# Layer 1's last scalings among layer 2's first products, in a written order

## The chip, the cores and the metric

The kernel runs on one core of a Trainium2 chip. A core has a matrix engine (TensorE, PE in the profile; its weight loads are PEld), a vector engine (VectorE, DVE), a scalar engine (ScalarE, ACT), a general engine (GpSimd, POOL) and a queue for transfers (SyncE, SP). Each engine works through its own queue in order and waits for the others by semaphores. The metric is the device time of one execution in microseconds (us).

## The reference

Four graph layers work on `x` of shape (8, 2048, 64) with one adjacency matrix of 2048 by 2048 nodes, each followed by a residual addition and a layer norm without weights. The change touches the end of layer 1 and layer 2:

```python
x = _layernorm(x + _L1_gnn_ref(x, ...))      # layer 1: a softmax over neighbours for each feature
# layer 2
A = (adj > 0); deg = A.sum(axis=1)
agg = einsum('ij,bjf->bif', A, x) / max(deg, 1)
out = relu(x @ W_self + b_self + agg @ W_neigh + b_neigh)
out = layernorm(out) * ln_gamma + ln_beta
x = _layernorm(x + out)
```

A layer norm here is a scale and a shift for each row of 64 values: x * rstd + nmr, with rstd and nmr worked out from the row's mean and variance.

## The kernel before

**Tiles.** The 2048 nodes lie in 16 tiles of 128 nodes. `X[:, t]` holds tile t: 128 partitions by 8 batches by 64 features. Nodes are sorted so that tiles 0 to 7 get their neighbour sums from products with the dense matrix `ET` ("by matrix"), and tiles 8 to 15 from gathered rows ("by list").

**End of layer 1 (L801 to L964).** The sums of a tile go to `finish` (L823), which divides on VectorE, adds to X and, when both tiles of a pair (2k, 2k+1) are done, calls `layer_norm` (L185). This takes the statistics on VectorE (`norm_stats`, L162: 8 `bn_stats`, then a chain of ten small instructions) and then scales on ScalarE (`normed`, L178): one activation of 128 by 64 for each tile and batch, 16 for a pair, at L183. Tiles 3 to 7 go through `add_rows` (L817), lists through `add_edges` (L946). The list tiles run from 15 down to 8, the matrix tiles up to 7, so that tiles 8 and 7 end last.

**Layer 2's first products (L1115 to L1133).** For each tile in the order of `turns` (0, 1, 2, 15, 14, 3, 4, 13, 12, 5, 6, 11, 10, 7, 9, 8): TensorE turns the tile in four transposes (`transposed`, L124) into a PSUM tile `pt`, ScalarE copies it to `xT` (L129), and TensorE multiplies it with the two weight matrices side by side (L1120) into a PSUM tile `py`. Half of that is x @ W_neigh, which ScalarE copies out as `y` (L1124). It goes to the table `ytab` in DRAM by SP (L1125), from which the lists' rows are gathered, and is split in three bf16 pieces `Y`: the high one is a cast on GpSimd (L1126), VectorE takes the remainder `rest` (L1130), the middle one is a cast of that on ScalarE (L1131), the low one a difference on GpSimd (L1132). The other half plus the biases becomes `S` (L1127, VectorE). At the end of each tile, `X[:, t]` gets layer 2's beta added (L1133, VectorE), since both the residual and the output need it later.

**Layer 2's main loop (L1280 to L1304).** It has 128 steps k, one for each pair of a matrix tile `it` and a tile `jt` of neighbours. A step issues three products with the pieces of Y (L1290), then what stands `beside` it: the weights of layer 3's heads are prepared at k = 2, 6, 10 and 14 (`prepare`, L1051: VectorE subtracts in place at L1055, TensorE multiplies and transposes at L1057 to L1061, VectorE copies out). Then it moves on the `chains` (L1174), generators that normalise finished tiles and end in `show` (L1213), which copies a tile on GpSimd (L1216) and stores it for layer 3. Between the steps lists are added (`add_edges`, L1262) and the next gathers are issued on GpSimd (`fetch`, L1253). The sum of tile 0 is complete at k = 15 and goes to `finish` (L1230).

**What sets the order.** Outside blocks marked `tc.manual_schedule(engines=...)` a planner orders each engine's instructions by its own estimate of when they can run, with earlier lines preferred. Inside such a block the order of each engine among the block's own instructions is that of the program. The planner may still put instructions from outside the block, also those of other blocks, between them. Before, L1115 to L1133 are in no such block, and the main loop is in one. PSUM has 8 banks: the seam uses 2 for `ps_m`, 2 for `pt` and 4 for two `py`.

Of the kernel before, what the change touches and what calls it, by code (L numbers as in the profile page):

```python
# [21 lines left out]
F32 = mybir.dt.float32  # L22
# [26 lines left out]
def kernel(ctx: ExitStack, tc: tile.TileContext, ins: dict, out: bass.AP):  # L49
    nc = tc.nc  # L50
    x, adj = ins["x"], ins["adj"]
    B, N, D = x.shape
    NT = N // P
    BD = B * D
    NP = B // 2
# [68 lines left out]
    def transposed(dst, src, psp):  # L124

        pt = psp.tile([P, NP, P], F32, name="pt")
        for p in range(NP):
            nc.tensor.transpose(pt[:, p], src[:, 2 * p:2 * p + 2, :].rearrange("p b d -> p (b d)"), ident)
        nc.scalar.copy(dst, pt)  # L129
# [32 lines left out]
    def norm_stats(chunks):  # L162

        n = len(chunks)
        st = small.tile([P, n, NP, 6], F32, name=f"st{n}")

        for c, v in enumerate(chunks):
            for a in range(NP):
                nc.vector.bn_stats(st[:, c, a], v[:, 2 * a:2 * a + 2, :].rearrange("p b d -> p d b"))
        triples = st.rearrange("p n a (k m) -> p (n a k) m", m=3)  # L170
        var, rstd, tmp, nmr = (small.tile([P, n * B], F32, name=f"ln_{k}{n}") for k in "vrtm")
        nc.vector.scalar_tensor_tensor(var, triples[:, :, 2], 1.0 / D, eps.to_broadcast(var.shape),
                                       op0=ALU.mult, op1=ALU.add)
        inv_sqrt(rstd, var, tmp)
        nc.vector.scalar_tensor_tensor(nmr, triples[:, :, 1], -1.0, rstd, op0=ALU.mult, op1=ALU.mult)  # L175
        return rstd, nmr

    def normed(chunks, stats):  # L178
        rstd, nmr = stats
        for c, v in enumerate(chunks):  # L180
            for b in range(B):
                k = c * B + b
                nc.scalar.activation(v[:, b], v[:, b], AF.Identity, scale=rstd[:, k:k + 1], bias=nmr[:, k:k + 1])  # L183
# [120 lines left out]
    def node_products(t0, wk, ps):  # L304
# [24 lines left out]
        for q, ph in enumerate(held):  # L329
# [40 lines left out]
                                   op0=ALU.is_equal, op1=ALU.mult)  # L370
# [184 lines left out]
    wk = adj_.enter_context(tc.tile_pool(name="l0k", bufs=2, reuse_waits="tile"))  # L555
# [220 lines left out]
    engines = {mybir.EngineType.PE, mybir.EngineType.Activation, mybir.EngineType.DVE, mybir.EngineType.Pool}  # L776
# [21 lines left out]

    with ExitStack() as l1:  # L801
        wp = l1.enter_context(tc.tile_pool(name="l1w", bufs=1, reuse_waits="tile"))
        wk = l1.enter_context(tc.tile_pool(name="l1k", bufs=2, reuse_waits="tile"))
        pa = l1.enter_context(tc.tile_pool(name="l1pa", bufs=8, space=PSUM, reuse_waits="tile"))
# [14 lines left out]
                                     start=(jt == 0 and q == 0), stop=(jt == NT - 1 and q == 2))  # L819

        done = set()

        def finish(it, po):  # L823
            for h in range(2):
                rec = wk.tile([P, HB * D], F32, name="rec")
                nc.vector.reciprocal(rec, po[h][:, 0])  # L826
                nc.vector.tensor_tensor(po[h][:, 1], po[h][:, 1], rec, ALU.mult)
                Xs = X[:, it, h * HB:(h + 1) * HB, :].rearrange("p b d -> p (b d)")
                nc.vector.tensor_tensor(Xs, po[h][:, 1], Xs, ALU.add)
            done.add(it)  # L830
            if it ^ 1 in done:
                layer_norm([X[:, t] for t in (it & ~1, it | 1)], wk)


        FIRST = 3
# [8 lines left out]
        rs_, rests = {}, {}  # L844
# [141 lines left out]
    ps_m = None  # L986
# [97 lines left out]
    with ExitStack() as l2:  # L1084
        wp = l2.enter_context(tc.tile_pool(name="l2w", bufs=1, reuse_waits="tile"))
        wk = l2.enter_context(tc.tile_pool(name="l2k", bufs=2, reuse_waits="tile"))
        ps_m = l2.enter_context(tc.tile_pool(name="l2pm", bufs=2, space=PSUM, reuse_waits="tile"))

        Wsn = wp.tile([P, 2, P], F32, name="Wsn")
        nc.gpsimd.memset(Wsn, 0.0)  # L1090
        for k, w in enumerate(("L2_gnn_W_self", "L2_gnn_W_neigh")):
# [6 lines left out]
        b2 = rows("b2", ins["L2_gnn_ln_beta"], wp)  # L1098
# [11 lines left out]
        turns = sorted(range(NT), key=lambda t: turns.index(t) if t in turns else NT)  # L1110
        with ExitStack() as turned:
            tk = turned.enter_context(tc.tile_pool(name="l2t", bufs=2, reuse_waits="tile"))
            ps = turned.enter_context(tc.tile_pool(name="l2ps", bufs=2, space=PSUM, reuse_waits="tile"))
            pa = turned.enter_context(tc.tile_pool(name="l2py", bufs=2, space=PSUM, reuse_waits="tile"))
            for t in turns:  # L1115
                xT = tk.tile([P, NP, P], F32, name="xT")
                transposed(xT, X[:, t], ps)
                py = pa.tile([P, NP, 2, P], F32, name="py")
                for p in range(NP):
                    nc.tensor.matmul(py[:, p].rearrange("p a n -> p (a n)"), xT[:, p],  # L1120
                                     Wsn.rearrange("p a n -> p (a n)"), start=True, stop=True)
                hi, mid, lo = (Y[:, t, k] for k in range(3))
                y = tk.tile([P, NP, P], F32, name="y", bufs=3)
                nc.scalar.copy(y, py[:, :, 1])  # L1124
                nc.sync.dma_start(ytab[t * P:(t + 1) * P, :], y.rearrange("p a n -> p (a n)"))  # L1125
                nc.gpsimd.tensor_copy(hi, y)  # L1126
                nc.vector.tensor_tensor(S[:, t].rearrange("p (q b) d -> p q b d", b=2), py[:, :, 0].rearrange("p q (b d) -> p q b d", d=D),  # L1127
                                        over(bsn, [P, NP, 2, D]), ALU.add)
                rest = tk.tile([P, NP, P], F32, name="rest", bufs=3)
                nc.vector.tensor_tensor(rest, py[:, :, 1], hi, ALU.subtract)  # L1130
                nc.scalar.copy(mid, rest)  # L1131
                nc.gpsimd.tensor_tensor(lo, rest, mid, ALU.subtract)  # L1132
# [146 lines left out]
        engines = {mybir.EngineType.PE, mybir.EngineType.Activation, mybir.EngineType.DVE, mybir.EngineType.Pool}  # L1279
        with tc.manual_schedule(engines=engines):  # L1280
            fetch(0)
            fetch(1)
            selection(0)
            selection(1)
            n = 0
            for k, (it, jt) in enumerate(steps):
                if jt == 0:
                    sums[it] = pa.tile([P, BD], F32, name="pa")
                for q in range(3):
                    nc.tensor.matmul(sums[it], ET[:, jt, it * P:(it + 1) * P], Y[:, jt, q].rearrange("p a n -> p (a n)"),  # L1290
                                     start=(jt == 0 and q == 0), stop=(jt == NT - 1 and q == 2))
                if jt == NT - 1:
                    finish(it)
                if k in beside:
                    f, *a = beside[k]
                    f(*a)
                for _ in range(2 if k % 2 == 0 else 1):
                    advance()
                while n < len(quads) and n * (len(steps) - LATE - EARLY) <= (k - LATE) * len(quads):
                    add_edges(n)  # L1300
                    fetch(n + 2)
                    n += 1
            while chains:
                advance()  # L1304
# [25 lines left out]
    with early, ExitStack() as heads:  # L1330
        wk = heads.enter_context(tc.tile_pool(name="f3s", bufs=2, reuse_waits="tile"))
# [258 lines left out]
        engines = {mybir.EngineType.PE, mybir.EngineType.Activation, mybir.EngineType.DVE, mybir.EngineType.Pool}  # L1590
        AHEAD = 8
        with tc.manual_schedule(engines=engines):
# [11 lines left out]
            for m in range(len(steps) // 2):  # L1604
                it, j = divmod(m, PER)
# [24 lines left out]
            t = NT - 1  # L1630
# [293 lines left out]
    with tc.If(bad > 0), ExitStack() as anyway:  # L1924
# [12 lines left out]
        X = main.tile([P, NT, B, D], F32, name="X")  # L1937
# [13 lines left out]
        with tc.tile_pool(name="adjp", bufs=3) as ap_, tc.tile_pool(name="adjps", bufs=4, space=PSUM) as aps:  # L1951
# [509 lines left out]
```

## Time and profile before

| | us |
|---|---|
| median of 3 runs | 1612.18 |
| lowest and highest run | 1601.11, 1620.49 |
| the profiled execution's own time | 1768.37 |
| its span | 1766.6 |
| last products of layer 1 end | 669.4 |
| first transpose for layer 2 | 669.3 |
| first product of layer 2 (L1120) | 684.5 |
| first product of the main loop (L1290) | 728.4 |
| last product of the main loop | 878 |

Times inside the profile count from the start of the span. A row of the timeline gives start, length, engine, line, operation, output and inputs, shape and count of merged instructions, and in brackets how long the engine had been idle and what released it. In merged rows the length covers all instructions of the row.

### The profile page before, as it was taken

How to read it: one execution, taken by the hardware profiler on the slowest of the kernel's cores; microseconds unless marked ns; L12 is line 12 of the kernel's file. 1: busy time of each engine (PE TensorE's matmuls, PEld its weight loads, DVE VectorE, ACT ScalarE, POOL GpSimd, SP SyncE). 2: the span in 40 equal slices, each digit the busy share in tenths (PEclk: the TensorE clock that was granted, in tenths of full speed). 3: DMA queues.
4: the chain of work that ended last, by engine and by line, in shares of the span. 5: the costliest groups of instructions: out<-in, count | busy, mean ns of one | idle time of the engine just before them, and what ended most of it. 6: DMA issues, size and time to landing. Idle time of an engine off the chain costs nothing.

```text
span 1766.6 us, 39998 instructions
## 1 busy us (share of the span) xinstructions
PE 1409.4 (80%) x16140; PEld 956.7 (54%) x16140; DVE 1165.4 (66%) x2846; ACT 884.2 (50%) x1843; POOL 790.0 (45%) x786
## 2 busy tenths in 40 slices
PE   4775567755899996989728999998989679889884
PEld 4764233322343334522227777777777567777773
DVE  6787578776985646655834666666666536656667
ACT  4553245558833225445634565656555324555564
POOL 1234666661235552656433333343333156666651
PEclk9965575676899998999958999999999879888997
DMA  5434767662247971366434565656565365666651
GB/s 166 126 127 131 211 214 232 179 195 82 102 167 262 328 273 43 128 176 182 123 90 106 151 178 152 172 154 167 161 161 153 89 202 167 179 174 177 181 163 45
DMA packets 159322, 285.71 MB, mean 162 GB/s; under 512 B 68986, under 2 KB 94586, under 8 KB 157050
## 3 DMA queue, kind: packets, MB, share of 16 engines
q0 software_dynamic: 56320, 190.10, 36.5%
q1 hardware_dynamic: 86168, 88.78, 16.8%
q10 hardware_dynamic: 16640, 4.20, 1.0%
q8 instruction: 129, 2.11, 0.5%
q14 instruction: 65, 0.53, 0.1%
HBM read 242.52 MB, written 40.48 MB: 160 GB/s over the span
## 4 chain that ended last, share of the span: by engine, by line
PE 50%; DVE 9%; ACT 6%; issue 4%; DMA 1%; POOL 1%; another core or an unknown queue 1%; SPq 0%; POOLq 0%; ACTq 0%; DVEq 0%
PE pscore L1388 10%; PE po L1413 6%; PE pa L817 6%; PE ps L1716 4%; PE po L1755 4%; PE pt L1693 3%; PE pa L946 2%; PE pscore L1351 2%; PE pa L1290 2%; PE py L1120 2%; PE pscore L1480 2%; PE pe L1686 2%; PE pt L1000 2%; ACT w L1391 1%; DVE w_mid L1394 1%
## 5 line engine op out<-in xcount | busy, mean ns | idle before, releaser
L218 POOL DMA_INDIRECT xs<-xtab,src x160 | 171.8, 1074 | 280.8 <-PE po L1413 241.6
L218 POOL DMA_INDIRECT hs<-ktab,src x160 | 158.5, 991 | 140.2 <-DMA utab<-hT 47.7
L218 POOL DMA_INDIRECT hs<-htab,src x160 | 157.1, 982 | 88.5 <-issue 43.3
L1388 PE MATMUL pscore<-U,xsT 64*128 64x64 f32 (+2 forms) x2560 | 165.8, 280 | 1.1 <-ACT xsT L1375 1.1
L1388 PEld LDWEIGHTS pscore<-U,xsT 64*128 64x128 f32 x2560 | 155.2, 193 | 5.2 <-ACT xsT L1375 1.3
L1391 ACT ACTIVATE w<-pscore 128x512 f32<-128x512 f32 (+1 forms) x128 | 75.8, 622 | 139.7 <-PE pscore L1388 139.3
L1394 DVE SCALAR_TENSOR_TENSOR w<-w,Sel 128x512 f32<-128x512 f32 (+1 forms) x128 | 89.3, 722 | 79.2 <-ACT w L1391 61.1
L183 ACT ACTIVATE X<-X,ln_m,ln_r 128x64 f32<-128x64 f32 x240 | 81.4, 427 | 73.5 <-DVE ln_m L175 59.5
L1755 PE MATMUL po<-hs,w 128*32 128x65 f32 x2048 | 89.4, 236 | 32.3 <-issue 23.4
L1716 PE MATMUL ps<-U,hsT 128*128 128x64 f32 x768 | 104.5, 287 | 8.8 <-issue 5.8
L1716 PEld LDWEIGHTS ps<-U,hsT 128*128 128x128 f32 x768 | 103.0, 210 | 9.8 <-issue 6.0
L218 POOL DMA_INDIRECT rs<-rtab,src x80 | 75.9, 949 | 69.9 <-PE pa L946 47.5
L613 DVE TENSOR_TENSOR hs<-hs,w 128x1024 f32<-128x1024 f32 x80 | 96.7, 1213 | 11.1 <-ACT w L603 6.0
L817 PE MATMUL pa<-R,ET 128*128 128x512 bf16 x440 | 101.6, 380 | 0.0
L826 DVE RECIPROCAL rec<-pa 128x256 f32<-128x256 f32 x32 | 54.4, 1734 | 65.7 <-PE pa L946 41.6
L1755 PEld LDWEIGHTS po<-hs,w 128*32 128x32 f32 x2048 | 71.5, 119 | 45.1 <-issue 33.3
L1413 PE MATMUL po<-w,xs 128*64 128x64 f32 (+1 forms) x2048 | 84.4, 230 | 9.6 <-DVE o L1397 5.6
L218 POOL DMA_INDIRECT rs<-ytab,src x80 | 76.2, 953 | 35.0 <-issue 17.4
L1694 ACT COPY hsT<-pt 128x512 f32<-128x512 f32 x96 | 52.5, 586 | 77.8 <-remote 45.0
L1413 PEld LDWEIGHTS po<-w,xs 128*64 128x64 f32 x2048 | 71.4, 139 | 35.5 <-DVE w L1394 20.4
L1803 ACT ACTIVATE z<-z,ln_m,ln_r 128x64 f32<-128x64 f32 x240 | 83.4, 432 | 12.9 <-DVE ln_m L1791 12.9
L1290 PE MATMUL pa<-Y,ET 128*128 128x512 bf16 x384 | 89.4, 382 | 0.0
(673 smaller groups left out, 3355.3 us busy)
## 6 DMA issues: line engine op xcount, KB each, us to landing
at<-in_adj SPq DMA_DIRECT2D x16, 1024.0 KB
R<-itab SPq DMA_DIRECT2D x60, 256.0 KB
rtab<-r SPq DMA_DIRECT2D x16, 512.0 KB
ptab<-hp SPq DMA_DIRECT2D x16, 384.0 KB
hi<-ptab SPq DMA_DIRECT2D x16, 384.0 KB
htab<-H SPq DMA_DIRECT2D x16, 260.0 KB
own<-htab SPq DMA_DIRECT2D x16, 260.0 KB
ktab<-hb SPq DMA_DIRECT2D x16, 260.0 KB
```

The costliest lines, as they stand in the source:

```text
L183: nc.scalar.activation(v[:, b], v[:, b], AF.Identity, scale=rstd[:, k:k + 1], bias=nmr[:, k:k + 1])
L218: nc.gpsimd.indirect_dma_start(out=dst, out_offset=None, in_=table[:, :], in_offset=bass.IndirectOffsetOnAxis(ap=src[:, it, s, g:g + 1], a ...
L613: nc.vector.tensor_tensor(wx, wx, along(w[:, rows_]), ALU.mult)
L817: nc.tensor.matmul(po[h].rearrange("p a f -> p (a f)"), ET[:, jt, it * P:(it + 1) * P], piece[jt][q][:, h * BD:(h + 1) * BD], start=(jt == ...
L1290: nc.tensor.matmul(sums[it], ET[:, jt, it * P:(it + 1) * P], Y[:, jt, q].rearrange("p a n -> p (a n)"), start=(jt == 0 and q == 0), stop=( ...
L1388: nc.tensor.matmul(pscore[:, k_, f0:f0 + HN * ni].rearrange("p (h i) -> p h i", i=ni), xsT[half, p], Us[it][half, p, :, i0:i0 + ni], start ...
L1391: nc.scalar.activation(w.rearrange("p k a h i -> p k (a h i)"), pscore[:, :, 0:NP * HN * ni], AF.Exp)
L1394: nc.vector.scalar_tensor_tensor(wt, wt, 3.0e38, edge, op0=ALU.min, op1=ALU.mult)
L1413: nc.tensor.matmul(po[half, p, :, a - blk * GB:b - blk * GB], xs[:, f0:f0 + D], w[:, k_, p, :, a - WINDOWS[s][0]:b - WINDOWS[s][0]], start ...
L1716: nc.tensor.matmul(pscore[:, g, 2 * p:2 * p + 2], hsT[:, g, p], U[:, p, :, node_block(g, k)], start=False, stop=(p == NP - 1))
L1755: nc.tensor.matmul(po[node_block(g, k), j, b], w[:, g, t], hs[:, g, t], start=(s == BEGIN[k] and b == 0), stop=(s == END[k] and b == B // ...
L1803: nc.scalar.activation(v, v, AF.Identity, scale=r, bias=n)
```

## The change

The pools and the order of the seam are rewritten:

- `finish` of layer 1 now calls `norm_stats` and `normed` itself. When the tile that completes a pair is in `LATE_NORMS` (6, 7, 8, 9), the statistics are taken as before, but the scalings are put off in the list `late`.
- The loop over `turns` stands in a `manual_schedule` block. It is cut into `turn_x` (transposes and copy), `both_products`, `top_piece` (y, its store, the high piece, S, the remainder) and `other_pieces` (middle and low piece). A step i issues `turn_x` for tile i+1, the products and top piece of tile i, and the other pieces of tile i-1. From the third step on it issues four of the put-off scalings, by turns on ScalarE and VectorE.
- `py` has three buffers in place of two (6 banks) and comes first in PSUM; `ps_m` is opened after the seam, no longer beside it.
- Beta is added to `X[:, turns[k]]` in step k of the main loop, for k from 0 to 15, after what stands beside the step.

The instructions are the same in kind and number but for 16 of the 32 put-off scalings, which go from ScalarE's activation to VectorE's `tensor_scalar`.

```diff
+    late = []
...
         done = set()
+        LATE_NORMS = (6, 7, 8, 9)
...
             if it ^ 1 in done:
-                layer_norm([X[:, t] for t in (it & ~1, it | 1)], wk)
+                pair = it & ~1, it | 1
+                pair_stats = norm_stats([X[:, t] for t in pair])
+                if it in LATE_NORMS:
+                    late.append((pair, pair_stats))
+                else:
+                    normed([X[:, t] for t in pair], pair_stats)
...
-        ps_m = l2.enter_context(tc.tile_pool(name="l2pm", bufs=2, space=PSUM, reuse_waits="tile"))
...
+            pa = turned.enter_context(tc.tile_pool(name="l2py", bufs=3, space=PSUM, reuse_waits="tile"))
             ps = turned.enter_context(tc.tile_pool(name="l2ps", bufs=2, space=PSUM, reuse_waits="tile"))
-            pa = turned.enter_context(tc.tile_pool(name="l2py", bufs=2, space=PSUM, reuse_waits="tile"))
-            for t in turns:
-                xT = tk.tile([P, NP, P], F32, name="xT")
-                transposed(xT, X[:, t], ps)
...
+            def turn_x(t):
+                xTs_[t] = tk.tile([P, NP, P], F32, name="xT")
+                transposed(xTs_[t], X[:, t], ps)
+
+            def both_products(t):
...
+            def top_piece(t):
+                py = pys.pop(t)
                 y = tk.tile([P, NP, P], F32, name="y", bufs=3)
                 nc.scalar.copy(y, py[:, :, 1])
                 nc.sync.dma_start(ytab[t * P:(t + 1) * P, :], y.rearrange("p a n -> p (a n)"))
-                nc.gpsimd.tensor_copy(hi, y)
+                nc.gpsimd.tensor_copy(Y[:, t, 0], y)
...
+                rest = rests[t] = tk.tile([P, NP, P], F32, name="rest", bufs=3)
+                nc.vector.tensor_tensor(rest, py[:, :, 1], Y[:, t, 0], ALU.subtract)
+
+            def other_pieces(t):
+                rest = rests.pop(t)
+                nc.scalar.copy(Y[:, t, 1], rest)
+                nc.gpsimd.tensor_tensor(Y[:, t, 2], rest, Y[:, t, 1], ALU.subtract)
+
+            scalings = [(t, k * B + b, b, stats_) for pair, stats_ in late for k, t in enumerate(pair) for b in range(B)]
+
+            def scale_late(on_dve):
+                t, c, b, (rstd, nmr) = scalings.pop(0)
+                v = X[:, t, b]
+                if on_dve:
+                    nc.vector.tensor_scalar(v, v, rstd[:, c:c + 1], nmr[:, c:c + 1], op0=ALU.mult, op1=ALU.add)
+                else:
+                    nc.scalar.activation(v, v, AF.Identity, scale=rstd[:, c:c + 1], bias=nmr[:, c:c + 1])
+
+            with tc.manual_schedule(engines=engines):
+                turn_x(turns[0])
+                for i, t in enumerate(turns):
+                    if i + 1 < NT:
+                        turn_x(turns[i + 1])
+                    both_products(t)
+                    top_piece(t)
+                    if i:
+                        other_pieces(turns[i - 1])
+                    for k in range(4):
+                        if i >= 2 and scalings:
+                            scale_late(k % 2)
+                other_pieces(turns[-1])
+
+        ps_m = l2.enter_context(tc.tile_pool(name="l2pm", bufs=2, space=PSUM, reuse_waits="tile"))
...
-                nc.vector.tensor_tensor(X[:, t], X[:, t], over(b2, [P, B, D]), ALU.add)
...
+                if k < NT:
+                    nc.vector.tensor_tensor(X[:, turns[k]], X[:, turns[k]], over(b2, [P, B, D]), ALU.add)
```

More of the change, by code (lines that the diff above doesn't have):

```diff
@@ L1110 @@
         turns = sorted(range(NT), key=lambda t: turns.index(t) if t in turns else NT)
+        engines = {mybir.EngineType.PE, mybir.EngineType.Activation, mybir.EngineType.DVE, mybir.EngineType.Pool}
         with ExitStack() as turned:
             tk = turned.enter_context(tc.tile_pool(name="l2t", bufs=2, reuse_waits="tile"))
+            pa = turned.enter_context(tc.tile_pool(name="l2py", bufs=3, space=PSUM, reuse_waits="tile"))
             ps = turned.enter_context(tc.tile_pool(name="l2ps", bufs=2, space=PSUM, reuse_waits="tile"))
-            pa = turned.enter_context(tc.tile_pool(name="l2py", bufs=2, space=PSUM, reuse_waits="tile"))
-            for t in turns:
-                xT = tk.tile([P, NP, P], F32, name="xT")
-                transposed(xT, X[:, t], ps)
-                py = pa.tile([P, NP, 2, P], F32, name="py")
+            xTs_, pys, rests = {}, {}, {}
+            def turn_x(t):
+                xTs_[t] = tk.tile([P, NP, P], F32, name="xT")
+                transposed(xTs_[t], X[:, t], ps)
+            def both_products(t):
+                xT = xTs_.pop(t)
+                py = pys[t] = pa.tile([P, NP, 2, P], F32, name="py")
                 for p in range(NP):
@@ L1121 @@
                                      Wsn.rearrange("p a n -> p (a n)"), start=True, stop=True)
-                hi, mid, lo = (Y[:, t, k] for k in range(3))
+            def top_piece(t):
+                py = pys.pop(t)
                 y = tk.tile([P, NP, P], F32, name="y", bufs=3)
@@ L1125 @@
                 nc.sync.dma_start(ytab[t * P:(t + 1) * P, :], y.rearrange("p a n -> p (a n)"))
-                nc.gpsimd.tensor_copy(hi, y)
+                nc.gpsimd.tensor_copy(Y[:, t, 0], y)
                 nc.vector.tensor_tensor(S[:, t].rearrange("p (q b) d -> p q b d", b=2), py[:, :, 0].rearrange("p q (b d) -> p q b d", d=D),
                                         over(bsn, [P, NP, 2, D]), ALU.add)
[L1129 to L1132, printed above, removed]
-                nc.vector.tensor_tensor(X[:, t], X[:, t], over(b2, [P, B, D]), ALU.add)
+                rest = rests[t] = tk.tile([P, NP, P], F32, name="rest", bufs=3)
[26 more added lines that the diff above has]
+        ps_m = l2.enter_context(tc.tile_pool(name="l2pm", bufs=2, space=PSUM, reuse_waits="tile"))
         gk = l2.enter_context(tc.tile_pool(name="l2g", bufs=8, reuse_waits="tile"))
```

## The prediction

> **What bounds the kernel now.** I read four views, from wide to narrow. First the page's row of engine shares and its chain of the work that ended last. They say that TensorE carries about half of the chain, and that layer 2's first products are 2% of it:
>
> ```profile
> PE 1409.4 (80%) x16140; PEld 956.7 (54%) x16140; DVE 1165.4 (66%) x2846; ACT 884.2 (50%) x1843; POOL 790.0 (45%) x786
> PE 50%; DVE 9%; ACT 6%; issue 4%; DMA 1%; POOL 1%; another core or an unknown queue 1%; SPq 0%; POOLq 0%; ACTq 0%; DVEq 0%
> ```
>
> A share of the whole span says little about one seam, so next the busy times by stretch, in two parts of the seam between the layers (columns: stretch, its length, then busy time of PE, PEld, DVE, ACT, POOL, the granted clock, DMA). In the first part TensorE does 1 us of 15; in the second it does 38 of 44:
>
> ```profile
> 669.30:684.40 15.10, 1.02 (x9) 0.78 (x7) 9.28 (x37) 11.21 (x34) 0.00 (x0) 0.70 0.01 3
> 684.40:728.40 44.00, 38.01 (x185) 32.00 (x186) 30.34 (x44) 24.03 (x44) 27.78 (x29) 0.95 0.23 85
> ```
>
> Then the timeline of the seam. These rows are ScalarE, TensorE and VectorE there (start, length, engine, line, work, count, idle before and its releaser):
>
> ```profile
> 669.29 1.04 PE L128 MATMUL pt<-ident,X 128*128 128x128 f32 x8
> 673.19 10.71 ACT L183 ACTIVATE X<-X,ln_m,ln_r 128x64 f32<-128x64 f32 x32 [15.16 <-DVE ln_m L175]
> 683.81 1.04 ACT L129 COPY xT<-pt 128x512 f32<-128x512 f32 x2
> 684.47 5.97 PE L1120 MATMUL py<-Wsn,xT 128*128 128x256 f32 x16 [14.15 <-ACT xT L129]
> ...
> 695.68 1.04 PE L128 MATMUL pt<-ident,X 128*128 128x128 f32 x8
> 697.57 3.72 PE L1120 MATMUL py<-Wsn,xT 128*128 128x256 f32 x16 [0.85 <-ACT xT L129]
> 701.12 1.04 PE L128 MATMUL pt<-ident,X 128*128 128x128 f32 x8
> ...
> 728.36 2.10 PE L1290 MATMUL pa<-Y,ET 128*128 128x512 bf16 x9
> ```
>
> Two tiles are already transposed at 670.3, but their copy out of PSUM stands on ScalarE behind layer 1's last 32 scalings, which wait for the statistics of the last tile. So TensorE idles 14.15 us. After that the tiles go in pairs, 701.12 - 695.68 = 5.44 us a pair: 1.0 us of transposes, 0.85 us waiting for ScalarE's copy, 3.55 us of products. From the first transpose to the first product of the main loop (L1290): 15.18 us, 5.81 us for the first pair, 7 x 5.44 us, in all 59.07 us.
>
> Last, the list of waits in and after the seam:
>
> ```profile
> PE py L1120 <- ACT xT L129: 20.1, 8, 14.1
> ACT y L1124 <- PE py L1120: 18.4, 16, 3.4
> POOL Xo L1216 <- ACT X L1157: 6.8, 1, 6.8
> ```
>
> The first is the idle time just told. The third is where the next margin lies: a copy on GpSimd, behind which gathers are queued, waits for tile 0's whole normalisation, and TensorE later idles 4.79 us (758.2 to 763.0) for those gathers.
>
> **What the Trainium skill says.** "TensorE: Matmul & The Clock Gate", the section on the clock gate: an idle window of about 3.4 us halves the clock until activity has lasted as long again. The trace agrees: the granted clock is 0.70 in the idle part, and the first 16 products take 5.97 us, later ones 3.72. "PSUM — Partial Sum Buffer", the section on bank collisions: two engines may not read one bank in the same partitions at once, so ScalarE's y and VectorE's S from one product tile go one after the other. The trace agrees: y ends at 688.85, S starts at 688.88. "SBUF — State Buffer", the section on who interferes with whom: a VectorE instruction with two SBUF inputs, or in a 2-port mode, shuts out a GpSimd one that reads SBUF, and the other way round. The trace agrees in size: the addition of beta (L1133) takes 0.69 or 1.03 us, GpSimd's cast (L1126) 0.61 or 0.95.
>
> **The change part by part.**
>
> *Scalings deferred.* Tile 7 completes pair (6,7), tile 8 completes pair (8,9); both are in the late set, and no other pair is. So exactly the 32 activations of the 10.71 us row leave ScalarE's queue ahead of the copies. They come back in eight steps (the third to the tenth tile), two on ScalarE at 10.71/32 = 0.335 us and two on VectorE at 0.31 us (median of the like scaling at L1167). The two engines have room, see below. Tiles 8, 9, 6 and 7 are scaled in steps 3-4, 5-6, 7-8 and 9-10, before their transposes are issued (tile 6 with step 10, the others later), so no transpose waits for them. If that cover were gone, 16 x 0.335 = 5.4 us of ScalarE would lie open.
>
> *The start.* The first copy can run at once, ScalarE being idle since 658: transpose 0.5 us, copy 0.59, two hand-overs of 0.1, so products begin about 1.3 us after the first transpose instead of 15.18. But VectorE is busy with tile 7's finish and its statistics until 677.5, the first remainder (`rest`) stands behind that, and in the new fixed order ScalarE's second step waits for that remainder ahead of the copy for the fourth tile. Products of the first three tiles end near 677.3; the fourth starts at 677.8 if the remainder slips in between the statistics, at about 680-681 if not. I take a bubble of 2.0 us, bounds 0 and 3.5.
>
> *The steps.* The transposes of tile i+1 go ahead of the products of tile i, so the 0.85 us wait is covered by 1.8 us of products. Per tile: TensorE 0.52 + 1.78 = 2.30 us. ScalarE three copies or casts at 0.52 (back to back) + 0.67 = 2.2. VectorE 0.6 + 0.6 + 0.62 = 1.8. GpSimd 0.61 to 0.95 for the cast + 1.16 for the difference = 1.8 to 2.1. TensorE is the longest, so 16 x 2.30 = 36.8 us. The ends: 2.30, and 2.72 if collisions of VectorE's scalings with GpSimd eat the 0.2 to 0.5 us of room. The third buffer for the products covers the time until VectorE has read a tile (about 2.1 us after its products).
>
> Sum of the stage: 1.3 + 2.0 + 36.8 = 40.1 us against 59.07, a gain of **19.0 us**.
>
> *Beta moved.* 16 additions of 0.605 us (two back to back take 1.29) leave the seam, where they stood on VectorE beside TensorE's work and cost nothing, and go into the first 16 steps of the main loop, each of which is only 0.65 us of TensorE. There they are not covered: the preparation of a head (L1055 to L1063) is issued at steps 2, 6, 10 and 14, and TensorE's L1057 waits for VectorE's L1055, which now stands behind four additions. From one L1057 to the next took 3.03 us (730.30 to 733.33). Now: copies done after 1.05 us, four additions 2.42, two L1055 0.5, hand-over 0.1, together 4.1 us. So three times 1.05, and about 0.4 at the first one, whose PSUM bank was held by the last product tile until its remainder is read: **3.6 us** back. Bounds: 1 us (some additions hoisted by the planner) and 6 us (additions slowed to 1.03 by GpSimd).
>
> *Tile 0's chain.* Two additions more stand before tile 0's first statistics are turned into a scale: 1.2 us later, and the 4.79 us wait grows by as much: **1.2 us**, bounds 0 and 3. Behind it on GpSimd's queue are the gathers, and TensorE waits for those. SP's stores of y keep their place: each is issued after its copy and none is waited for before the loop's gathers, which GpSimd still begins after its last low piece.
>
> Net: 19.0 - 3.6 - 1.2 = **14.2 us** of the profiled execution's 1768.37 us (span 1766.6). That execution is 9.7% longer than the runs' median of 1612.18, so I shrink the gain by the same ratio, 0.912: 13 us, **1599 us**. The runs of before lie within 1601 to 1620, so about 1% is what can be told from no change.
>
> **The rivals.** (a) *Nothing is given back*: VectorE's additions fit into waits that TensorE has anyway and there is no bubble; gain 21 x 0.912 = 19, 1593 us. For it: TensorE waits 4.79 us at 758-763 in any case, and a delay before that could vanish in it; against: that wait hangs on tile 0's chain, which is late by as much. (b) *The round of four engines sets the pace*: still 2.72 us a tile, 43.5 + 3.3 = 46.8, gain 12.3 - 4.8 = 7.5, times 0.912 is 7: 1605 us. For it: fixed order, strict queues, GpSimd at 1.8 to 2.1 of 2.3. (c) *Slower*: the fixed order closes a ring in ScalarE's queue: products, y, GpSimd's cast, remainder, middle piece, scalings, the copy for the tile after next, products. Its links add to about 6.3 us (1.8 + 0.6 + 0.95 + 0.7 + 0.6 + 0.67 + 0.6 + 0.4 of hand-overs) and it spans three tiles, so 2.1 us a tile, under 2.30. If a wait ties it to one tile and a half, a step is 4.2 us: 67 + 3 + 4.8 against 59, a loss of 16, 1627 us. It decides from (59.07 - 3.3 - 4.8)/16 = 3.2 us a step. (d) *It doesn't do what it says*: the planner merges the new order with what surrounds it so that the copies still stand late; 1612.
>
> **How the numbers follow.** Forecast 0.50, (a) 0.22, (b) 0.15, (c) 0.08, (d) 0.05. Below 1596 lie most of (a) and the forecast's better end: faster 0.31; slower takes (c) and the spread of the runs: 0.10; same 0.59. The range, 1587 to 1612, goes from (a) less the spread of a median to (b) and (d).
>
> **What would show it.** Right: products start within 3 us of the first transpose; none of the 32 scalings ahead of the first copy; TensorE's wait for the copy near zero from the fourth tile on; 2.3 us a tile; L1290 begins near 710; L1057 spaced near 4.1 us with waits on VectorE. Wrong: a tile at 2.7 us or more, scalings grown by collisions, or a wait for gathers that grows by more than 3 us.

## The result and the profile after

The changed kernel takes 1594.73 us (median of 12 runs, 1590.73 to 1602.76), the kernel before 1605.66 us (12 runs beside it, 1600.52 to 1620.49). The ratio is 0.992, with a 95% interval of 0.9895 to 0.9944: 9 to 17 us faster, 12.8 us in the middle (the two medians alone are 10.9 us apart). The prediction said 13 us and 1599 us; it counted the 1599 from a median of 1612.18 us over three runs.

The kernel before was profiled in an execution of 1768 us, which is as long as its runs beside all the experiments below (medians 1765 to 1779 us) but about 160 us longer than the runs compared here, with 41 us of the difference in layer 0 and 116 us behind layer 2, where nothing was changed, so the traces are compared by stretch and not by their whole spans.

These are the sums for layer 1, for the seam and for layer 2's main loop, of before and then of after (columns as in the prediction; the last one is GB/s moved):

```profile
442.50:669.40 226.90, 218.53 (x1154) 84.58 (x1154) 155.62 (x320) 88.54 (x174) 94.99 (x99) 0.97 0.62 220
669.40:728.40 59.00, 38.93 (x194) 32.68 (x193) 39.52 (x81) 35.24 (x77) 27.78 (x29) 0.88 0.18 64
728.40:878.40 150.00, 134.72 (x611) 46.69 (x613) 92.60 (x321) 77.57 (x208) 88.74 (x97) 0.95 0.58 165
```

```profile
401.20:628.10 226.90, 216.28 (x1152) 83.63 (x1151) 154.59 (x320) 88.58 (x174) 95.86 (x99) 0.98 0.61 220
628.10:670.30 42.20, 37.06 (x192) 31.90 (x192) 34.99 (x83) 29.16 (x62) 24.48 (x29) 0.96 0.26 94
670.30:818.60 148.30, 131.01 (x610) 45.61 (x610) 99.13 (x333) 77.18 (x208) 89.85 (x98) 0.95 0.57 166
```

Layer 1 is 226.9 us in both. The change shows in the second row, the seam: 59.0 us became 42.2 us, while TensorE's busy time in it fell only from 38.9 to 37.1 us. The main loop of layer 2 has 148.3 us in place of 150.0.

The timeline of the seam in the changed kernel, TensorE first and then one step of ScalarE (`xT` is the copy of the next tile, `y` and `Y` the pieces of this and the last one, L1158 two of the put-off scalings):

```profile
632.59 1.77 PE L128 MATMUL pt<-ident,X 128*128 128x128 f32 x8 [4.52 <-DVE X L831]
634.23 2.94 PE L1131 MATMUL py<-Wsn,xT 128*128 128x256 f32 x8
...
646.10 1.93 PE L1131 MATMUL py<-Wsn,xT 128*128 128x256 f32 x8
647.87 0.60 PE L128 MATMUL pt<-ident,X 128*128 128x128 f32 x4
648.31 1.89 PE L1131 MATMUL py<-Wsn,xT 128*128 128x256 f32 x8
...
670.32 2.12 PE L1330 MATMUL pa<-Y,ET 128*128 128x512 bf16 x9 [0.40 <-DVE rest L1143]
```

```profile
645.91 0.59 ACT L1137 COPY y<-py 128x512 f32<-128x512 f32 x1
646.39 0.62 ACT L1147 CAST Y<-rest 128x512 bf16<-128x512 f32 x1
646.91 0.77 ACT L1158 ACTIVATE X<-X,ln_m,ln_r 128x64 f32<-128x64 f32 x2
647.59 0.57 ACT L129 COPY xT<-pt 128x512 f32<-128x512 f32 x1
648.12 0.59 ACT L1137 COPY y<-py 128x512 f32<-128x512 f32 x1
```

The block of 32 scalings is gone, and a tile takes 648.31 - 646.10 = 2.2 us with no wait for a copy. ScalarE has no gap in such a step. New is the first row: TensorE idles 4.52 us *before* the first transposes, where before it idled 14.15 us behind them. It waits for tile 7's last addition on VectorE (L831).

Behind the seam, TensorE at the preparations of the heads in the main loop and at the later wait for gathers, then VectorE at the same preparations. Before:

```profile
728.36 2.10 PE L1290 MATMUL pa<-Y,ET 128*128 128x512 bf16 x9
730.30 0.38 PE L1057 MATMUL pm<-wb 128*128 128x128 f32 x2
733.33 0.39 PE L1057 MATMUL pm<-wb 128*128 128x128 f32 x2
...
739.38 0.38 PE L1057 MATMUL pm<-wb 128*128 128x128 f32 x2
763.00 5.24 PE L1270 MATMUL pa<-rs,self__5913 128*32 128x512 f32 x8 [4.79 <-DMA rs<-ytab,src]
```

After:

```profile
672.27 0.38 PE L1064 MATMUL pm<-wb 128*128 128x128 f32 x2
676.72 0.49 PE L1064 MATMUL pm<-wb 128*128 128x128 f32 x2 [1.26 <-DVE wb L1062]
681.15 0.49 PE L1064 MATMUL pm<-wb 128*128 128x128 f32 x2 [1.13 <-DVE wb L1062]
685.43 0.49 PE L1064 MATMUL pm<-wb 128*128 128x128 f32 x2 [0.98 <-DVE wb L1062]
707.59 4.80 PE L1310 MATMUL pa<-rs,self__5900 128*32 128x512 f32 x8 [3.45 <-DMA rs<-ytab,src]
```

```profile
673.32 2.91 DVE L1338 TENSOR_TENSOR X<-X,b 128x512 f32<-128x512 f32 x4
676.15 0.52 DVE L1062 TENSOR_SCALAR wb<-wb 64x64 f32<-64x64 f32 x2
```

The preparations are 4.3 to 4.45 us apart (3.03 before), and the second to fourth wait for the subtraction that stands behind four additions of beta. The fourth comes 15.11 us after the loop's first product, before it was 11.02. The wait for gathers ends 37.27 us after that product, before 34.64: so 2.6 us of the seam's 16.7 are given back by then, and 14.1 us are left at that point.

At the end of the main loop those 2.6 us are no longer to be seen: from the end of layer 1 to there the rows above give 209.0 and 190.5 us, 18.5 us less, and the changed kernel of experiment 5 gives 193.3. But the loop's length differs by 3.4 us between two profiles of one and the same kernel (148.7 us in experiment 6, 152.1 in experiment 12). So the traces don't show how much of the 2.6 us reaches the whole time.

### The profile page after: what moved, and what is told of

Read it like the earlier page. It is cut to its first block, busy times and chain, and to the rows that moved or that the text cites. A ratio compares the mean times of both kernels' runs of the same rounds, so it can differ in the third digit from the quotient of the medians.

```text
span 1590.5 us, 39997 instructions
## 1 busy us (share of the span) xinstructions
PE 1320.9 (83%) x16140; PEld 911.1 (57%) x16140; DVE 1167.3 (73%) x2862; ACT 884.6 (56%) x1827; POOL 787.3 (50%) x786
## 4 chain that ended last, share of the span: by engine, by line
PE 48%; DVE 12%; ACT 5%; issue 3%; POOL 2%; DMA 1%; SPq 0%; POOLq 0%; ACTq 0%; DVEq 0%
PE pscore L1430 10%; PE pa L818 6%; PE po L1455 6%; PE pscore L1393 4%; PE pt L1007 3%; PE pa L953 3%; PE ps L1758 3%; PE po L1797 2%; PE pscore L1522 2%; PE pt L1735 2%; ACT z L1197 2%; PE pa L889 1%; PE py L1131 1%; ACT X L1197 1%; POOL hs L218 1%
## 5 line engine op out<-in xcount | busy, mean ns | idle before, releaser
L218 POOL DMA_INDIRECT xs<-xtab,src x160 | 168.0, 1050 | 233.6 <-PE po L1455 203.9
L218 POOL DMA_INDIRECT hs<-htab,src x160 | 156.8, 980 | 53.5 <-issue 45.1
L1430 PE MATMUL pscore<-U,xsT 64*128 64x64 f32 (+2 forms) x2560 | 161.8, 276 | 1.6 <-ACT xsT L1417 1.1
L1430 PEld LDWEIGHTS pscore<-U,xsT 64*128 64x128 f32 x2560 | 151.1, 190 | 5.6 <-ACT xsT L1417 1.3
L1433 ACT ACTIVATE w<-pscore 128x512 f32<-128x512 f32 (+1 forms) x128 | 79.7, 624 | 88.1 <-PE pscore L1430 85.9
L183 ACT ACTIVATE X<-X,ln_m,ln_r 128x64 f32<-128x64 f32 x208 | 70.7, 427 | 58.5 <-DVE ln_m L175 56.2
L818 PE MATMUL pa<-R,ET 128*128 128x512 bf16 x440 | 101.6, 380 | 0.0
L1758 PE MATMUL ps<-U,hsT 128*128 128x64 f32 x768 | 95.5, 271 | 1.1 <-ACT hsT L1736 1.1
L1758 PEld LDWEIGHTS ps<-U,hsT 128*128 128x128 f32 x768 | 94.2, 195 | 1.5 <-ACT hsT L1736 1.3
L1417 ACT COPY xsT<-pt 128x1024 f32<-128x1024 f32 x80 | 80.9, 1011 | 10.1 <-PE pt L1007 10.1
L818 PEld LDWEIGHTS <-ET 128*128 128x128 fp8e4 x480 | 45.0, 98 | 71.1 <-issue 19.3
L889 PE MATMUL pa<-R,ET 128*128 128x512 bf16 x264 | 60.8, 388 | 24.9 <-ACT R L876 14.6
```

Source lines behind the costliest of these rows:

```text
L218: nc.gpsimd.indirect_dma_start(out=dst, out_offset=None, in_=table[:, :], in_offset=bass.IndirectOffsetOnAxis(ap=src[:, it, s, g:g + 1], a ...
L818: nc.tensor.matmul(po[h].rearrange("p a f -> p (a f)"), ET[:, jt, it * P:(it + 1) * P], piece[jt][q][:, h * BD:(h + 1) * BD], start=(jt == ...
L889: nc.tensor.matmul(sums[it][h].rearrange("p a f -> p (a f)"), ET[:, jt, it * P:(it + 1) * P], piece[jt][q][:, h * BD:(h + 1) * BD], start= ...
L1417: nc.scalar.copy(unflipped(xsT), pt.rearrange("p k s a n -> p k (s a) n"))
L1430: nc.tensor.matmul(pscore[:, k_, f0:f0 + HN * ni].rearrange("p (h i) -> p h i", i=ni), xsT[half, p], Us[it][half, p, :, i0:i0 + ni], start ...
L1433: nc.scalar.activation(w.rearrange("p k a h i -> p k (a h i)"), pscore[:, :, 0:NP * HN * ni], AF.Exp)
```

## The experiments

All ran in three groups, each beside the kernel before. Each seam and each wait below is read from one profiled execution; experiments 9 and 10 have no other, and so no ratio. "Seam" is the time from the end of layer 1's last products to the main loop's first product, read from each profile. It is steadier than the total: the changed kernel's seam was 42.25 us in its first profile and 43.46 us in the second group.

**1. The order without the deferral.**

```diff
-        LATE_NORMS = (6, 7, 8, 9)
+        LATE_NORMS = ()
```

> The changed kernel with an empty late set: the fixed order of the seam, its three product buffers and the moved beta stay, the 32 scalings are issued at the end of layer 1 as before. Seam means from the end of layer 1's last products to the first product of the main loop: 58.9 us before, 42.3 us changed. Theory (the deferral is what frees the first copies): the scalings stand ahead of the copies again, first products 11 to 13 us after the first transposes, seam about 53 to 55 us, and with the beta additions in the main loop the time is within 3 us of the kernel before. Rival (the fixed order alone does it, the planner letting the copies pass): seam 42 to 44 us, the time of the changed kernel.

Measured: seam 51.5 us, ratio 0.9962 (0.9934 to 0.999). The copies stand behind the block again:

```profile
670.31 10.71 ACT L183 ACTIVATE X<-X,ln_m,ln_r 128x64 f32<-128x64 f32 x32 [15.17 <-DVE ln_m L175]
680.93 1.04 ACT L129 COPY xT<-pt 128x512 f32<-128x512 f32 x2
```

First products come 10.5 us after the first transposes; then a tile takes 2.17 us. The rival falls: the order alone doesn't free the copies. But the theory put the gain too low: with the order, three product buffers and the beta additions out of the seam, the seam is 7.4 us shorter than before and the total 2 to 12 us. The first product comes 15.0 us after the end of layer 1, as before, so all of the 7.4 us is in the pace.

**2. The deferral without the order.** In the kernel before, the loop over `turns` stays as it was, under the planner, and gets at its end:

```diff
+                for k in range(4):
+                    if i >= 2 and scalings:
+                        scale_late(k % 2)
```

> The kernel before with only the deferral: the 32 scalings put off and issued four a tile from the third tile on, in the loop that the planner orders; two product buffers, beta added in the seam. Theory (deferral gives the start, the order gives the pace): no block of 32 ahead of the first copy, products start about 2 us after the first transposes, then pairs of 5.4 us or more, seam 46 to 49 us, 8 to 12 us faster than before. Rival 1 (deferral alone does everything): seam 42 us or less. Rival 2 (without the order the planner gathers the scalings ahead of the copies all the same): seam 55 us or more.

Measured: seam 50.9 us, ratio 0.9941 (0.9922 to 0.996), 10 us faster. The planner put eight scalings ahead of the first copy after all, and these wait for statistics:

```profile
672.83 2.76 ACT L1130 ACTIVATE X<-X,ln_m,ln_r 128x64 f32<-128x64 f32 x8 [15.16 <-DVE ln_m L175]
675.50 1.04 ACT L129 COPY xT<-pt 128x512 f32<-128x512 f32 x2
```

Products start 9.0 us after the transposes, and the pace is 2.6 us a tile. So the truth lies between the theory and its second rival. The gains seem to add up: 7.4 us for the order and 8.0 us for the deferral make 15.4 us, and both together gave 58.91 - 43.46 = 15.45 us (experiment 5). But the parts don't match. Up to the first product the gains are 0 (order), 6.2 (deferral) and 8.7 us (both), and behind it 7.4, 1.7 and 6.8 us: the deferral frees the whole start only with the order, and the put-off scalings take back some of the pace. That the sums agree is luck.

**3. Beta moved, nothing else.** The kernel before with L1133 taken out and the changed kernel's two lines put into the main loop.

> The kernel before with only the beta additions moved to the first 16 steps of the main loop. Theory (they delay the heads' preparations, for which TensorE waits): seam unchanged at 58 to 59 us, from the first product of the main loop to the fourth preparation 15 us in place of 11.0, time 3 to 5 us slower than before. Rival (hidden, since TensorE waits for tile 0's gathers later in any case): the same 15 us, but the time from the first product to the end of that later wait, 34.6 us before, grows by less than 1 us.

Measured: seam 58.7 us; the fourth preparation 15.7 us after the loop's first product; the wait for gathers ends 3.1 us later than in the kernel before, counted from that product (37.7 against 34.6). Ratio 1.001 (0.9994 to 1.0026). The stretch behaves as the theory says, and the rival's "less than 1 us" is missed; the total, 1.8 us slower with an interval of -1 to 5 us, can't tell a loss from none.

**4. The transposes' banks first.**

```diff
-            pa = turned.enter_context(tc.tile_pool(name="l2py", bufs=3, ...))
             ps = turned.enter_context(tc.tile_pool(name="l2ps", bufs=2, ...))
+            pa = turned.enter_context(tc.tile_pool(name="l2py", bufs=3, ...))
```

> The changed kernel with the order of the two PSUM pools of the seam exchanged: the transposes' two banks first, the products' six behind them. Theory (in the changed kernel the first transposes wait 4.5 us for banks that tile 7's last sums still hold): transposes start at once, seam 38 to 39 us in place of 42.3, 3 to 4 us faster. Rival (the start is gated by VectorE, whose remainder for the first tile comes after tile 7's statistics, and the fourth product waits instead): seam 41 us or more, no gain beyond 1 us.

Measured: seam 43.8 us, ratio 0.9926 (0.9907 to 0.9944). The rival holds. The transposes do start at once, which shows that the 4.52 us are a wait for banks. But the time is lost again at the second and the fourth product. TensorE, then VectorE:

```profile
667.10 1.97 PE L1131 MATMUL py<-Wsn,xT 128*128 128x256 f32 x8 [0.28 <-issue]
670.45 1.97 PE L1131 MATMUL py<-Wsn,xT 128*128 128x256 f32 x8 [0.96 <-DVE X L831]
677.89 3.43 PE L1131 MATMUL py<-Wsn,xT 128*128 128x256 f32 x8 [2.87 <-DVE S L1140]
```

```profile
673.99 0.17 DVE L175 SCALAR_TENSOR_TENSOR ln_m<-st,ln_r 128x16 f32<-128x16 f32 x1
674.22 1.29 DVE L1338 TENSOR_TENSOR X<-X,b 128x512 f32<-128x512 f32 x2
675.42 0.68 DVE L1140 TENSOR_TENSOR S<-py,bs 128x512 f32<-128x512 f32 x1
676.02 0.68 DVE L1143 TENSOR_TENSOR rest<-py,Y 128x512 f32<-128x512 f32 x1
```

The first remainder comes behind tile 7's finish, its statistics and two additions of beta that the planner pulled ahead. That is the bubble that the prediction had described for the changed kernel.

**5. The changed kernel again,** as a reading for the second group.

> The changed kernel itself, beside the others of this group on the same chip. Seam 42.3 us as in its first profile, of which 4.5 us are TensorE's wait for tile 7's banks; fourth head's preparation 15.1 us after the main loop's first product; about 13 us faster than before (the first comparison gave 9 to 17).

Measured: ratio 0.9934 (0.9904 to 0.9964), seam 43.46 us, wait for the banks 4.52 us, fourth preparation at 15.12 us. The seam is 1.2 us longer than in its first profile.

**6. The heads' subtractions in the seam.** The two lines of L1055 leave `prepare`, become `centre(h)`, and stand in the fixed order:

```diff
                         if i >= 2 and scalings:
                             scale_late(k % 2)
+                    if 10 <= i < 10 + HN:
+                        centre(i - 10)
```

> The changed kernel with the in-place subtractions of the four heads' weights taken out of the preparation and issued on VectorE in the seam, one head a step in steps 10 to 13, where no scaling stands. Theory (TensorE waits for these subtractions because they stand behind four beta additions): the preparations are 3.0 to 3.3 us apart again, the fourth one 11 to 12 us after the main loop's first product in place of 15.1, seam unchanged within 0.5 us, 3 to 4 us faster than the changed kernel. Rival (the time is needed for tile 0's chain and its gathers anyway): the preparations are back at 3 us, but the wait for tile 0's gathers grows by as much, and the time from the first product to the end of that wait stays within 1 us of 37.3.

Measured: seam 42.8 us, and TensorE no longer waits at the preparations:

```profile
711.18 0.38 PE L1067 MATMUL pm<-wb 128*128 128x128 f32 x2
714.21 0.38 PE L1067 MATMUL pm<-wb 128*128 128x128 f32 x2
...
720.27 0.38 PE L1067 MATMUL pm<-wb 128*128 128x128 f32 x2
```

They are 3.03 us apart, the fourth at 11.04 us. The wait for gathers ends at 33.4 us and a short second one at 35.0, in place of 37.2 and 38.9 in experiment 5. Ratio 0.9897 (0.9869 to 0.9925), medians 1747.18 against 1754.28 us for the changed kernel in the same group. The theory holds for the stretch: the additions cost because they stand ahead of subtractions that TensorE waits for.

**7. The last statistics in the fixed order.** Banks first as in 4; the statistics of pair (6,7) are issued in steps 0 to 3, behind each step's remainder; the scalings start at step 4.

> The changed kernel with the transposes' PSUM banks first, and with the statistics of the pair (6,7) issued inside the fixed order, in steps 0 to 3 behind the remainder of each step; the scalings start in step 4, tiles 6 and 7 ahead of 8 and 9. Theory (once the banks are free early, the fourth product waits because VectorE's S and remainder of the first tile stand behind these statistics and the chain of small instructions): the wait of 2.9 us ahead of the fourth product shrinks below 1 us, seam 39 to 40.5 us in place of 43.8 with the banks alone and 42.3 in the changed kernel. Rival (VectorE is then late in steps 0 to 3 by the same 3 us and the wait only moves): seam 42 us or more.

Measured: seam 44.5 us, ratio 0.993 (0.9904 to 0.9957). The wait ahead of the fourth product is gone, but it has only moved to the seventh:

```profile
677.99 1.89 PE L1134 MATMUL py<-Wsn,xT 128*128 128x256 f32 x8
...
684.05 0.60 PE L128 MATMUL pt<-ident,X 128*128 128x128 f32 x4
688.07 2.16 PE L1134 MATMUL py<-Wsn,xT 128*128 128x256 f32 x5 [3.42 <-ACT xT L129]
```

The seam is what the rival said. VectorE's work in the first steps didn't get less, it grew: two of the chain's small instructions, 0.17 us each in the changed kernel, took 1.02 and 1.17 us and ended 0.03 us after a difference on GpSimd. Part of the wait also comes from this version's own order. The copy that the seventh product waits for stands on ScalarE behind two scalings of tile 6, and these wait 1.30 us for the statistics just moved; with tiles 8 and 9 scaled first, as in the changed kernel, that part might not have come. This was not tried.

**8. Everything together.** 4, 6 and 7, with two of the beta additions in the seam's last steps.

> The banks first, the last statistics in the fixed order, the four subtractions in seam steps 10 to 13, the first two beta additions in the seam's last two steps and the other 14 in steps 2 to 15 of the main loop. If both theories hold: seam 39 to 40.5 us, fourth preparation 11 to 12 us after the main loop's first product, 5 to 7 us faster than the changed kernel. If the rivals hold: within 2 us of the changed kernel.

Measured: seam 43.2 us, ratio 0.992 (0.9892 to 0.9949), preparations 3.03 us apart, but the first one at 3.64 us instead of 1.95, so the fourth at 12.7. VectorE is now late at the end of the seam: the loop's first product waits 3.27 us for the last remainder, 0.40 us in 6. The ratio is within 2 us of the changed kernel's: no better than 6 alone.

**9. All put-off scalings on ScalarE.**

```diff
-                            scale_late(k % 2)
+                            scale_late(False)
```

> The changed kernel with all 32 put-off scalings on ScalarE, four a step in steps 2 to 9. Theory (ScalarE with two scalings a step takes 2.17 us, just what TensorE takes, so it is at its edge): these eight steps take 2.17 + 0.67 = 2.8 us each, seam 5 us longer, about 48 us. Rival (ScalarE has room because TensorE's end times are modelled, or the third product buffer takes it up): seam within 1.5 us of the changed kernel's 42.3 to 43.5.

Measured: seam 47.2 us. A step with four scalings takes 2.81 us, and TensorE waits again for the copy:

```profile
687.75 1.99 PE L1131 MATMUL py<-Wsn,xT 128*128 128x256 f32 x8 [0.39 <-ACT xT L129]
690.56 1.99 PE L1131 MATMUL py<-Wsn,xT 128*128 128x256 f32 x8 [0.38 <-ACT xT L129]
```

The theory holds: with two scalings a step ScalarE was at its edge. At four scalings a step VectorE's half of them is needed; fewer a step over more steps, all on ScalarE, was not tried.

**10. Two product buffers in place of three.** `bufs=2` for `l2py`.

> The changed kernel with two product buffers instead of three. Theory (VectorE has read a tile about 2.1 us after its products, and a third buffer covers that): with two buffers each product waits for the remainder two tiles back, which is ready 2.1 us after that tile's products while TensorE needs 2.6 us to come round, so the pace of 2.17 us holds in the later steps, and only the first steps suffer; seam at most 3 us longer. Rival (the third buffer carries the whole gain in pace): about 2.7 us a tile, seam 50 us or more.

Measured: seam 45.1 us. From the third tile on most tiles take 2.17 us, as with three. The loss is at the ends: the pools lie otherwise, so the second tile's transposes wait 4.41 us for L831, and the main loop's first product waits 2.12 us for the last remainder, 0.40 us with three. The rival falls: the third buffer doesn't carry the pace.

**11. Beta left in the seam.** One addition a step behind the remainder, none in the main loop.

> The changed kernel with the beta additions left in the seam, one a step behind the remainder, none in the main loop. Theory (VectorE's 1.2 us a step plus 0.75 for two scalings leave 0.2 us, an addition takes 0.6): the eight steps with scalings take 2.5 us instead of 2.17, seam 2 to 4 us longer, preparations 3.03 us apart again, sum within 1.5 us of the changed kernel. Rival (buffers take up the lag, later steps have 0.9 us of room): seam unchanged within 1 us, 3 to 4 us faster than the changed kernel.

Measured: seam 52.1 us, 8.6 us longer than the changed kernel's and far outside both expectations; ratio 0.9957 (0.9941 to 0.9974). VectorE with GpSimd's low piece, then TensorE:

```profile
695.35 0.68 DVE L1167 TENSOR_TENSOR X<-X,b 128x512 f32<-128x512 f32 x1
695.95 1.41 DVE L1156 TENSOR_SCALAR X<-X,ln_r,ln_m 128x64 f32<-128x64 f32 x2
696.16 1.15 POOL L1148 TENSOR_TENSOR Y<-rest,Y 128x512 bf16<-128x512 f32 x1 [0.91 <-ACT Y L1147]
```

```profile
703.68 0.33 PE L128 MATMUL pt<-ident,X 128*128 128x128 f32 x1 [0.72 <-DVE X L1156]
705.79 0.45 PE L128 MATMUL pt<-ident,X 128*128 128x128 f32 x1 [1.78 <-DVE X L1156]
```

In the changed kernel (its first profile) the low piece and two scalings were:

```profile
644.97 1.16 POOL L1148 TENSOR_TENSOR Y<-rest,Y 128x512 bf16<-128x512 f32 x1
645.65 0.75 DVE L1156 TENSOR_SCALAR X<-X,ln_r,ln_m 128x64 f32<-128x64 f32 x2
```

Two scalings took 1.41 us where they had taken 0.75. With GpSimd idle they take 0.53 us, as those at 708.48 and 713.70 us of this run do. So the changed kernel already paid for meeting the low piece, but only its tail: the first scaling waits until it ends. Here the added 0.6 us shifts the second scaling onto the whole of it. In both runs the scaling that meets the piece ends 0.05 to 0.06 us after it, step for step. The Trainium skill, "SBUF — State Buffer", section "Who interferes with whom", says that a `tensor_scalar` can run in a mode that takes the port pair shared with GpSimd, and that of the two the one that starts first keeps the pair for its whole instruction; these ends agree.

A step then takes 3.1 us, all of it VectorE's, and the transposes of a late tile (tile 6) come to wait for its scalings, so that two steps take 6.7 and 4.3 us. Against the changed kernel of experiment 5 the wait for gathers ends earlier after the loop's first product, 35.6 us instead of 37.2, but 7.0 us later after the end of layer 1 (87.6 against 80.7 us). So moving beta out was better than this place for it, in spite of what it costs later. The totals can't confirm that: the two intervals overlap.

**12. Version 6 once more,** in more rounds.

> The version with the heads' subtractions in seam steps 10 to 13, once more and in more rounds, since it came out fastest: ratio to the kernel before 0.987 to 0.993 (the changed kernel had 0.9934 on the same chip), seam 42 to 43.5 us, fourth preparation at 11.0 us. If the earlier lead was the spread of the runs: 0.992 to 0.995.

Measured: ratio 0.9899 (0.9861 to 0.9938), seam 43.5 us, fourth preparation at 11.04 us. Both readings, 0.9897 and 0.9899, are below the changed kernel's 0.992 and 0.9934, but the intervals overlap. What is shown is the stretch: about 3.8 us less before the gathers arrive, with a seam of the same length.

## Why the prediction was right, step by step

*Scalings deferred*: right. All 32 left the head of ScalarE's queue and came back four a step. Experiment 1 shows that the block held the copies, experiment 9 that ScalarE couldn't have taken four of them a step. That no transpose waits for its scalings was right but for one wait of 0.27 us (tile 6).

*The start*: wrong in kind, and off in size. The transposes were to start at once and a bubble of 2.0 us to come at the fourth product. In fact they wait 4.52 us, since their PSUM banks now lie where tile 7's sums were; the bubble is then absent, because VectorE is done with tile 7 by the same time. The prediction listed the moved pools and didn't ask which earlier tile had their banks. From the end of layer 1's products to the first product of the seam, 6.2 us passed, against 1.3 + 2.0 predicted. Experiment 4 shows the predicted bubble (2.87 us) once the banks are free, and 0.96 us more at the second product, which then waits for L831 itself.

*The steps*: right in mechanism. TensorE sets the pace at 2.17 us a tile, with ScalarE just as full in the steps with scalings; 2.30 was predicted, with 2.72 as the bad end. The sum has no term for the lower clock after the idle time, though the prediction had told of it: the first eight products took 2.94 us, at a granted clock of 0.67 from 634.2 to 637.2 us, later ones 1.89 at 1.00. From the first product to the main loop it was 36.1 us in all, where 36.8 was said. The whole seam was put at 40.1 us and measured 42.25; its gain at 19.0 and measured 16.7.

*Beta moved*: right. The period was predicted at 4.1 us and measured 4.28 to 4.45; up to the fourth preparation the loss is 4.1 us, where 3.6 was said. The 0.4 us at the first preparation did not come: it lies 1.95 us behind the loop's first product, as before. Each period lost more instead, since four additions took 2.5 to 2.9 us, not 2.42, and the copies ahead of them 1.25 us in two of three periods, not 1.05. Experiment 6 removes the loss by the cause that was named.

*Tile 0's chain*: the sign was wrong. These rows are VectorE before, then after:

```profile
741.25 0.29 DVE L1058 COPY G<-pm 128x128 f32<-128x128 f32 x1 [3.20 <-PE pa L1290]
743.17 0.75 DVE L1232 SCALAR_TENSOR_TENSOR S<-pa,r_deg,S 128x512 f32<-128x512 f32 x1
```

```profile
687.29 0.74 DVE L1272 SCALAR_TENSOR_TENSOR S<-pa,r_deg,S 128x512 f32<-128x512 f32 x1
```

The wait for gathers was to grow by 1.2 us; it shrank from 4.79 to 3.45 us. The chain starts later, but by less than TensorE: tile 0's `finish` comes 17.0 us after the loop's first product (687.29 - 670.32) against 14.8 (743.17 - 728.36), while the fourth preparation moved by 4.1. In the kernel before, the copies of the fourth preparation had themselves come late (741.25, though its first product had ended by 739.8), and tile 0's finish stood behind them; that lateness is not there now. (Why they were late then is not shown.) So the two losses together are 2.6 us at the end of that wait, against 4.8 predicted. Rival (a), that a delay vanishes in the wait, was right in part.

The sum, 14.2 us, met the 14.1 us at the end of that wait because two errors of 2.3 and 2.2 us cancel. That is luck, and so is the place where it was read: at the end of the main loop the traces show 18.5 us. The shrinking by 0.912 was not grounded: layer 1 takes 226.9 us in both profiles and the changed seam 42.25 or 43.46 us, so a saving here shouldn't scale with the whole time. The runs' 9 to 17 us can't tell 13 from 14. Rivals (b) and (c) fall by the pace of 2.17 us, (d) by the ScalarE rows.

## What to carry to other kernels

A block of work that waits for the last result of a stage should not stand ahead of the next stage's first, independent work in the same in-order queue; put it between later steps, and check how much room each engine has in such a step, since here four scalings a step on one engine were too many. When work is moved off a stage into a loop, look at what the loop's other instructions on that engine release: the additions of 0.6 us left the preparations at 3.03 us when nothing waited behind them (experiment 6), and cost 1.3 to 1.4 us each time a subtraction that TensorE waited for stood behind four of them. When pools of PSUM are moved, ask who had those banks last.

## What was not expected of the hardware

Two small scalings on VectorE took 0.53 us with GpSimd idle, 0.75 us where the first met the end of GpSimd's low piece, and 1.41 us where the second met the whole of it. One more addition of 0.6 us a step was enough to move them from the second case to the third, and with the waits of tile 6's transposes behind it the seam grew by 8.6 us. A VectorE instruction of 0.17 us took 1.17 us in the same way (experiment 7). A sum of durations shows none of this: what counted was which instruction of the other engine they fell on.
